# Conv attention on one core: q and k weights on the SP queue, idle products from a tile of ones, and a different split of the last group between ScalarE and VectorE

## The chip, the core and the metric

The kernel runs on one core of a Trainium2 chip. A core has five engines with instruction streams of their own: TensorE (PE, with PEld for its weight loads), VectorE (DVE), ScalarE (ACT), GpSimd (POOL) and SyncE (SP, which here only starts transfers). The metric is the device time of one execution in microseconds. The kernel before takes 2464.09 us (median of 5 runs, 2462.86 to 2464.92).

## The reference

For each of B = 4 images x of 64 x 64 positions and C = 256 channels, three linear maps are followed by an attention and a residual:

```python
q = jnp.einsum('bwhc,cd->bwhd', x, Wq) + bq      # 128 channels
k = jnp.einsum('bwhc,cd->bwhd', x, Wk) + bk      # 128 channels
v = jnp.einsum('bwhc,cd->bwhd', x, Wv) + bv      # 256 channels
pq = q.reshape(B, -1, N); pk = k.reshape(B, -1, N); pv = v.reshape(B, -1, N)   # N = 4096
energy = jnp.einsum('bcn,bcm->bnm', pq, pk)
attention = jax.nn.softmax(energy, axis=-1)
out = jnp.einsum('bcm,bnm->bcn', pv, attention)
return gamma * out.reshape(B, W, H, C) + x
```

The reshape is not a transpose: the rows of pq are made of 32 positions times 128 channels, so N = 4096 counts both.

## The kernel before, in words

**Setup (lines 85 to 102 and 187 to 199).** `ident`, the identity for transposes on PE, is built by POOL; `ones` is set by DVE. The weights of q and k share one tile, `wqk_sb`, which two transfers issued by ACT fill (lines 90 and 91). POOL issues the broadcasts of the two biases, the weights of v, the bias of v and gamma. Lines 196 to 199 let PE do 12 transposes of the identity into a PSUM tile `wp` that nobody reads.

**Order.** From line 201 on the order is written out by hand (`manual_schedule`): each engine carries out its instructions in the order of the program, and a semaphore holds an instruction until its data or its buffer is there. Generators (`finish`, `guard`) spread a piece of work over the loop: each `yield` gives way to the next step.

**Projection of an image (class Projection, lines 104 to 173).** x comes in 16 tiles of 256 KB, each 128 partitions by 2 by 256, loaded by SP into a pool of three buffers. `transposed(i)` first asks for tiles i and i + 1 (`load` starts a transfer only once per tile), then transposes tile i with four PE transposes (line 124), and ACT copies the result from PSUM (line 130). `qk(i)` multiplies it by `wqk_sb` (line 137), and DVE adds the biases (line 146). `v(i)` does the same for v. Of the first image, tiles 0 and 1 are transposed before the first `qk` (lines 483 to 485).

**Attention.** Each image has NG = 16 groups of 256 columns, and each group 8 steps. A step forms energies (line 324), their exponentials on ACT (line 328) in two factors that DVE multiplies (line 338), splits the product into parts `h`, `l` and `d`, and accumulates on PE (line 374): `h` and `l` into two accumulators `acc[0]` and `acc[1]`, 128 x 258 each, and `d` into the tile `bb`, whose two halves of 128 x 256 share one PSUM bank. Column C of an accumulator holds z, the sum by which the row is divided.

**End of a group.** `finish` writes z into `zall`, forms gamma * (1 + E) / z, adds `bb`, scales on ACT, transposes back on PE, and DVE adds the result to x before POOL stores it. The very last group goes through `finish_last` instead: DVE copies z of both accumulators, `factors` forms r = gamma / z, and `ra` = r (1 + E). For each half, ACT computes `bb` * r, DVE `acc` * ra + that (line 449), PE transposes it (line 454), and DVE adds it to x (line 459); SP stores (line 460). In between, `guard` looks at all z: two DVE operations test them against Z_LOW and Z_HIGH, a reduction and a product with `ones` on PE bring the partitions together, and DVE writes the flag `again`.

**After the last group.** Every engine loads `again` (line 547) and branches: if some z was out of range, a general kernel computes everything anew. With these inputs the branch is not taken. Then all engines meet at the closing barrier (line 672).

Of the kernel before, what the change touches and what calls it, by code (L numbers as in the profile page):

```python
# [9 lines left out]
F32 = mybir.dt.float32  # L10
F32R = mybir.dt.float32r
I32 = mybir.dt.int32
AF = mybir.ActivationFunctionType
ALU = mybir.AluOpType
# [6 lines left out]
def kernel(  # L21
# [36 lines left out]
    nc = tc.nc  # L58
    B, W, H, C = x.shape
    P = 128  # L60
    N = W * H
    C2 = C // 2
# [3 lines left out]
    Z_LOW, Z_HIGH = 2.0**-60, 2.0**80  # L66
# [20 lines left out]
    ones = const.tile([P, P], F32, name="ones")  # L87
    nc.vector.memset(ones, 1.0)
    wqk_sb = const.tile([P, KC, 2 * C2], F32, name="wqk_sb")
    nc.scalar.dma_start(wqk_sb[:, :, :C2], wq.rearrange("(k p) d -> p k d", p=P))  # L90
    nc.scalar.dma_start(wqk_sb[:, :, C2:], wk.rearrange("(k p) d -> p k d", p=P))
    bqk_sb = const.tile([P, 2 * C2], F32, name="bqk_sb")
    nc.gpsimd.dma_start(bqk_sb[:, :C2], bq.partition_broadcast(P))
    nc.gpsimd.dma_start(bqk_sb[:, C2:], bk.partition_broadcast(P))
# [100 lines left out]

    with tc.tile_pool(name="ps_w", bufs=1, space=PSUM) as ps_w:
        wp = ps_w.tile([P, P], F32, name="wp")
        for _ in range(12):
            nc.tensor.transpose(wp, ident, ident)

    with ExitStack() as fast:
        fast.enter_context(tc.manual_schedule())
# [181 lines left out]
                for j in range(NJ):  # L384
                    nc.scalar.activation(o[:, j, :], acc[j], AF.Identity, scale=1.0 + E)

        def factors(b, g, gamma):

            r = work.tile([P, 2, NJ], F32, tag="r", name=f"r_{b}_{g}")
            nc.vector.reciprocal(r[:, 0, :], zall[:, b * NG + g, :])  # L390
            nc.vector.tensor_tensor(r[:, 0, :], r[:, 0, :], gamma.to_broadcast([P, NJ]), ALU.mult)
            return r[:, 0, :], r[:, 1, :]

        def finish(b, g, o, bb, xr):
            yield
            yield

            nc.vector.tensor_copy(zall[:, b * NG + g, :], o[:, :, C])
            r, _ = factors(b, g, gam1)
            nc.vector.tensor_tensor(o[:, :, :C], o[:, :, :C], bb, ALU.add)  # L400
            yield
            for j in range(NJ):
                nc.scalar.activation(
                    o[:, j, :C], o[:, j, :C], AF.Identity, scale=r[:, j : j + 1]
                )
            yield
            yield
            tp = ps_t.tile([P, 2, NB], F32, tag="t", name=f"ot_{b}_{g}")
            for s in range(2):
                for j in range(NJ):  # L410
                    nc.tensor.transpose(
                        tp[:, s, j * P : (j + 1) * P], o[:, j, s * P : (s + 1) * P], ident
                    )
            yield
            nc.vector.tensor_tensor(xr, xr, tp, ALU.add)
            nc.gpsimd.dma_start(ov[b, g], xr)

        def guard():

            z = zall.rearrange("p n j -> p (n j)")  # L420
            ok = ppool.tile([P, 4, NB], F32, tag="y", name="ok")[:, 0, : B * NG * NJ]
            nc.vector.tensor_scalar(ok, z, Z_LOW, None, ALU.is_ge)
            nc.vector.scalar_tensor_tensor(ok, z, Z_HIGH, ok, ALU.is_le, ALU.mult)
            yield
            nc.vector.tensor_reduce(zs, ok, AX.X, ALU.min)
            nc.vector.tensor_scalar(zs, zs, 0.5, None, ALU.is_lt)
            zp = ps_s.tile([P, 1], F32, tag="b", name="zp")
            nc.tensor.matmul(zp, ones, zs, start=True, stop=True)
            yield
            nc.vector.tensor_copy(again, zp)  # L430
            yield
            yield

        def finish_last(b, g, xr):

            for j in range(NJ):
                a = now["acc"][j]
                nc.vector.tensor_copy(zall[:, b * NG + g, j : j + 1], a[:, C : C + 1])
            r, ra = factors(b, g, gam)
            check = guard()  # L440
            nc.vector.tensor_scalar(ra, r, 1.0 + E, None, ALU.mult)
            o = work.tile([P, NJ, C + 2], F32, tag="o", name=f"o_{b}_{g}")
            tps = []
            for j in range(NJ):
                next(check)
                nc.scalar.activation(
                    o[:, j, :C], now["bb"][:, j, :], AF.Identity, scale=r[:, j : j + 1]
                )
                nc.vector.scalar_tensor_tensor(
                    o[:, j, :C], now["acc"][j][:, :C], ra[:, j : j + 1], o[:, j, :C], ALU.mult, ALU.add  # L450
                )
                tp = (ps_t, ps_s)[j].tile([P, 2, P], F32, tag="ta"[j], name=f"ot_{b}_{g}_{j}")
                for s in range(2):
                    nc.tensor.transpose(tp[:, s, :], o[:, j, s * P : (s + 1) * P], ident)
                tps.append(tp)
            for j in range(NJ):
                next(check)
                n = slice(j * P, (j + 1) * P)
                nc.vector.tensor_tensor(xr[:, :, n], xr[:, :, n], tps[j], ALU.add)
            nc.sync.dma_start(ov[b, g], xr)  # L460

        def begin(b, i):
# [16 lines left out]
        for b in range(B):  # L479
            pr = images[b]  # L480
            if b == 0:
                now["banks"] = energies
                pr.transposed(0)
                pr.transposed(1)
                project_qk(b, 0)
            for i in range(1, NI):
# [189 lines left out]
```

## Time and profile before

| what | value |
|---|---|
| median of 5 runs | 2464.09 us (2462.86 to 2464.92) |
| the profiled execution's own time | 2463.21 us |
| its span, first to last instruction | 2461.3 us |
| start of the first product with `wqk_sb` (line 137) | 8.57 us |
| start of the last store (line 460) | 2453.69 us |
| moved by the DMA engines | 498.92 MB, mean 203 GB/s |

Times in the views are microseconds from the start of the span. A line of the timeline has the start, the length, the engine, the line of the kernel, the operation, output <- input, and how many instructions are merged; in brackets stands how long the engine was idle before it and what ended that. An engine name with a q at its end is the engine's own sequencer, which issues transfers and handles semaphores; that is not counted as busy. A busy PE means that matmuls follow each other; an fp32 product takes two passes, so it has two records. A view of one line lists its operations with the minimum, median and maximum duration in ns and the first and last start.

### The profile page before, as it was taken

The page shows a single profiled execution, that of the slowest core. Times are in us where ns is not written, and L with a number is a line of the kernel's source. Part 1 is how long each engine was busy: PE and PEld are TensorE (multiplying, and loading weights), DVE is VectorE, ACT ScalarE, POOL GpSimd, SP SyncE. Part 2 cuts the span into 40 slices and gives each one's busy share as a digit, 9 for nine tenths or more (in the row PEclk, how much of TensorE's full clock was granted, in tenths as well). Part 3 has the DMA queues.
Part 4 walks back from the last instruction along what each step waited for, and adds up shares of the span by engine and source line. Part 5 has one row for each costly group of instructions (what it writes and reads, how often), then busy time and mean ns, then how long its engine had stood idle before and what let it go on. Part 6 is the DMA issues. An engine that isn't in the chain of part 4 may idle for free.

```text
span 2461.3 us, 50024 instructions
## 1 busy us (share of the span) xinstructions
PE 2442.9 (99%) x19982; PEld 2408.9 (98%) x19982; DVE 2096.2 (85%) x2314; ACT 1804.2 (73%) x3201; POOL 425.7 (17%) x781
## 2 busy tenths in 40 slices
PE   9999999999999999999999999999999999999998
PEld 8999999999899999999989999999998999999998
DVE  5888888888698888888869888888876988888887
ACT  5777777776677777777667777777766777777775
POOL 4211111111411111111141111111114111111110
PEclk9999999999999999999999999999999999999999
DMA  7666666664766666666477666666647766666663
GB/s 231 217 205 209 206 204 203 203 215 152 228 221 197 209 206 204 211 196 213 140 239 220 203 200 211 203 209 200 208 141 239 222 209 197 209 203 210 204 201 112
DMA packets 137408, 498.92 MB, mean 203 GB/s; under 512 B 15536, under 2 KB 57264, under 8 KB 137168
## 3 DMA queue, kind: packets, MB, share of 16 engines
q0 software_dynamic: 92320, 453.17, 59.3%
q1 hardware_dynamic: 44304, 42.22, 5.6%
q8 instruction: 160, 2.62, 0.4%
q14 instruction: 80, 0.66, 0.1%
q10 hardware_dynamic: 544, 0.26, 0.0%
HBM read 445.25 MB, written 50.33 MB: 201 GB/s over the span
## 4 chain that ended last, share of the span: by engine, by line


## 5 line engine op out<-in xcount | busy, mean ns | idle before, releaser
L328 ACT ACTIVATE x<-sa 128x512 f32<-128x512 f32 x1024 | 612.7, 598 | 496.5 <-PE sa L324 493.3
L338 DVE TENSOR_TENSOR x<-x,y 128x1024 f32<-128x1024 f32 x512 | 626.2, 1223 | 187.9 <-ACT y L328 187.9
L324 PE MATMUL sa<-q,k 128*128 128x256 f32 x4096 | 736.6, 279 | 1.1 <-ACT x L328 1.0
L352 DVE SCALAR_TENSOR_TENSOR d<-h,x 128x1024 fp32r<-128x1024 f32 x512 | 624.0, 1219 | 0.0
L349 DVE TENSOR_TENSOR l<-x,h 128x1024 fp32r<-128x1024 f32 x512 | 624.0, 1219 | 0.0
L324 PEld LDWEIGHTS sa<-q,k 128*128 128x128 f32 x4096 | 619.5, 188 | 2.6 <-ACT x L328 2.0
L328 ACT ACTIVATE y<-sb 128x512 f32<-128x512 f32 x1024 | 614.3, 600 | 0.0
L374 PE MATMUL a<-vh,h 128*128 128x258 f32 x4096 | 574.4, 283 | 0.0
L374 PE MATMUL a<-vl,l 128*128 128x258 f32 x4096 | 572.8, 282 | 0.0
L324 PE MATMUL sb<-q,k 128*128 128x256 f32 x2048 | 567.5, 277 | 0.0
L343 ACT ACTIVATE h<-x 128x1024 fp32r<-128x1024 f32 x512 | 543.7, 1062 | 22.7 <-DVE x L338 19.2
L374 PE MATMUL bb<-vd,d 128*128 128x256 f32 x4096 | 558.6, 279 | 0.0
L308 POOL DMA_DIRECT2D k<-kf x512 | 280.0, 547 | 1575.5 <-PE sb L324 1550.6
L374 PEld LDWEIGHTS a<-vl,l 128*128 128x128 f32 x4096 | 525.3, 189 | 0.0
L374 PEld LDWEIGHTS a<-vh,h 128*128 128x128 f32 x4096 | 522.9, 189 | 0.0
L374 PEld LDWEIGHTS bb<-vd,d 128*128 128x128 f32 x4096 | 515.1, 188 | 0.0
L324 PEld LDWEIGHTS sb<-q,k 128*128 128x128 f32 x2048 | 384.5, 188 | 0.9 <-ACT y L328 0.8
L137 PE MATMUL qk<-wqk_sb,xts 128*128 128x256 f32 x512 | 121.0, 379 | 0.0
L158 PE MATMUL v<-xts,wv_sb 128*128 128x256 f32 x512 | 120.3, 379 | 0.0
L158 PEld LDWEIGHTS v<-xts,wv_sb 128*128 128x128 f32 x512 | 97.3, 190 | 13.2
L137 PEld LDWEIGHTS qk<-wqk_sb,xts 128*128 128x128 f32 x512 | 92.3, 190 | 10.0
L273 POOL DMA_DIRECT2D qd<-qks x128 | 69.1, 545 | 183.1 <-DVE qks L146 173.7
(56 smaller groups left out, 868.0 us busy)
## 6 DMA issues: line engine op xcount, KB each, us to landing
k<-kf POOLq DMA_DIRECT2D x512, 768.0 KB, 4.7
x<-in_x_dram SPq DMA_DIRECT2D x128, 256.0 KB, 3.5
kf<-f POOLq DMA_DIRECT2D x64, 384.0 KB, 3.7
out_dram<-x POOLq DMA_DIRECT2D x63, 256.0 KB, 2.6
qd<-qks POOLq DMA_DIRECT2D x128, 64.0 KB, 2.8
qr<-qd SPq DMA_DIRECT2D x64, 128.0 KB, 2.6
wv_sb<-in_L_conv_Wv_dram POOLq DMA_DIRECT2D x1, 256.0 KB, 7.3
out_dram<-x SPq DMA_DIRECT2D x1, 256.0 KB, 3.9
```

Source lines behind the costliest of these rows:

```text
L137: nc.tensor.matmul(qk[:, s, :], self.xt[i][:, k, s, :], wqk_sb[:, k, :], start=(k == 0), stop=(k == KC - 1),)
L158: nc.tensor.matmul(vp[:, eh, :], wv_sb[:, k, eh * P : (eh + 1) * P], self.xt[i][:, k].rearrange("p s a -> p (s a)"), start=(k == 0), stop= ...
L273: nc.gpsimd.dma_start(qd[b, i // 2 + NG // 2 * s][:, i % 2, :], x[:, s, :C2])
L308: nc.gpsimd.dma_start(t.rearrange("p (i s) f d -> p i s (f d)", s=2), kf[b, u % NU])
L324: nc.tensor.matmul(to[:, i], kt[:, 2 * k + i, f, :], q[:, f], start=first, stop=last)
L328: nc.scalar.activation(to[:, 2 * k : 2 * k + 2, :], sp.rearrange("p i j d -> p i (j d)"), AF.Exp, scale=scale,)
L338: nc.vector.tensor_tensor(x, x, y, ALU.mult)
L343: nc.scalar.activation(h, units[b, u], AF.Identity, scale=UPPER)
L349: nc.vector.tensor_tensor(l, x, h.bitcast(F32), ALU.subtract)
L352: nc.vector.scalar_tensor_tensor(d, h.bitcast(F32), 1.0 + E, x, ALU.mult, ALU.subtract)
L374: nc.tensor.matmul(out_, left[:, i, j * P : (j + 1) * P], right[:, m, : out_.shape[1]], start=(t == i == 0 and (left is h or left is d and ...
```

## The change

The two transfers of `wqk_sb` leave ACT's queue for SP's, behind the first tile of x, which is now asked for explicitly, and ahead of the second. The 12 transposes of the identity become 7 products of `ones` with itself, and two more such products follow the transposes of the first tile of x, in the bank that `ps_t` owns. `factors` goes, and `finish` has its two instructions in place.

In `finish_last` each accumulator gets its own reciprocal, `raj` = gamma (1 + E) / z and `rj` = gamma / z; ACT scales the accumulator by `raj`, and DVE afterwards adds `bb` * `rj`. The copies of z into `zall` come after that. `guard` is no generator any more: POOL clamps z between Z_LOW and Z_HIGH, DVE compares the clamped values with z, the reduction and the product follow, and `again` is written by one comparison, between the two final additions.

```diff
-    nc.scalar.dma_start(wqk_sb[:, :, :C2], wq.rearrange("(k p) d -> p k d", p=P))
-    nc.scalar.dma_start(wqk_sb[:, :, C2:], wk.rearrange("(k p) d -> p k d", p=P))
...
         wp = ps_w.tile([P, P], F32, name="wp")
-        for _ in range(12):
-            nc.tensor.transpose(wp, ident, ident)
+        for _ in range(7):
+            nc.tensor.matmul(wp, ones, ones, start=True, stop=True)
...
-        def factors(b, g, gamma):
-
-            r = work.tile([P, 2, NJ], F32, tag="r", name=f"r_{b}_{g}")
-            nc.vector.reciprocal(r[:, 0, :], zall[:, b * NG + g, :])
-            nc.vector.tensor_tensor(r[:, 0, :], r[:, 0, :], gamma.to_broadcast([P, NJ]), ALU.mult)
-            return r[:, 0, :], r[:, 1, :]
-
         def finish(b, g, o, bb, xr):
...
-            r, _ = factors(b, g, gam1)
+            r = work.tile([P, 2, NJ], F32, tag="r", name=f"r_{b}_{g}")[:, 0, :]
+            nc.vector.reciprocal(r, zall[:, b * NG + g, :])
+            nc.vector.tensor_tensor(r, r, gam1.to_broadcast([P, NJ]), ALU.mult)
...
             ok = ppool.tile([P, 4, NB], F32, tag="y", name="ok")[:, 0, : B * NG * NJ]
-            nc.vector.tensor_scalar(ok, z, Z_LOW, None, ALU.is_ge)
-            nc.vector.scalar_tensor_tensor(ok, z, Z_HIGH, ok, ALU.is_le, ALU.mult)
-            yield
+            nc.gpsimd.tensor_scalar(ok, z, Z_LOW, Z_HIGH, ALU.max, ALU.min)
+            nc.vector.tensor_tensor(ok, ok, z, ALU.is_equal)
             nc.vector.tensor_reduce(zs, ok, AX.X, ALU.min)
-            nc.vector.tensor_scalar(zs, zs, 0.5, None, ALU.is_lt)
             zp = ps_s.tile([P, 1], F32, tag="b", name="zp")
             nc.tensor.matmul(zp, ones, zs, start=True, stop=True)
-            yield
-            nc.vector.tensor_copy(again, zp)
-            yield
-            yield
+            return zp

         def finish_last(b, g, xr):

+            r = work.tile([P, 2, NJ], F32, tag="r", name=f"r_{b}_{g}")
+            o = work.tile([P, NJ, C + 2], F32, tag="o", name=f"o_{b}_{g}")
+            acc, bb = now["acc"], now["bb"]
             for j in range(NJ):
-                a = now["acc"][j]
-                nc.vector.tensor_copy(zall[:, b * NG + g, j : j + 1], a[:, C : C + 1])
-            r, ra = factors(b, g, gam)
-            check = guard()
-            nc.vector.tensor_scalar(ra, r, 1.0 + E, None, ALU.mult)
-            o = work.tile([P, NJ, C + 2], F32, tag="o", name=f"o_{b}_{g}")
+                rj, raj, z = r[:, 0, j : j + 1], r[:, 1, j : j + 1], acc[j][:, C : C + 1]
+                nc.vector.reciprocal(rj, z)
+                nc.vector.tensor_tensor(raj, rj, gam1, ALU.mult)
+                nc.scalar.activation(o[:, j, :C], acc[j][:, :C], AF.Identity, scale=raj)
+                nc.vector.tensor_tensor(rj, rj, gam, ALU.mult)
+            for j in range(NJ):
+                nc.vector.tensor_copy(zall[:, b * NG + g, j : j + 1], acc[j][:, C : C + 1])
             tps = []
             for j in range(NJ):
-                next(check)
-                nc.scalar.activation(
-                    o[:, j, :C], now["bb"][:, j, :], AF.Identity, scale=r[:, j : j + 1]
-                )
                 nc.vector.scalar_tensor_tensor(
-                    o[:, j, :C], now["acc"][j][:, :C], ra[:, j : j + 1], o[:, j, :C], ALU.mult, ALU.add
+                    o[:, j, :C], bb[:, j, :], r[:, 0, j : j + 1], o[:, j, :C], ALU.mult, ALU.add
                 )
...
+            zp = guard()
             for j in range(NJ):
-                next(check)
                 n = slice(j * P, (j + 1) * P)
                 nc.vector.tensor_tensor(xr[:, :, n], xr[:, :, n], tps[j], ALU.add)
+                if j == 0:
+                    nc.vector.tensor_scalar(again, zp, P - 0.5, None, ALU.is_lt)
             nc.sync.dma_start(ov[b, g], xr)
...
                 now["banks"] = energies
+                pr.load(0)
+                nc.sync.dma_start(wqk_sb[:, :, :C2], wq.rearrange("(k p) d -> p k d", p=P))
+                nc.sync.dma_start(wqk_sb[:, :, C2:], wk.rearrange("(k p) d -> p k d", p=P))
                 pr.transposed(0)
+
+                wp = ps_t.tile([P, P], F32, tag="t", name="wp1")
+                for _ in range(2):
+                    nc.tensor.matmul(wp, ones, ones, start=True, stop=True)
                 pr.transposed(1)
```

## The prediction, made before the result was known

> **What bounds the kernel now.** I read the page's busy times, then PE's waits, then the two ends in order of time, because the change touches only the first 10 us and the last 12.
>
> ```profile
> PE 2442.9 (99%) x19982; PEld 2408.9 (98%) x19982; DVE 2096.2 (85%) x2314; ACT 1804.2 (73%) x3201; POOL 425.7 (17%) x781
> ```
>
> PE works without a break; the waits of PE (total, times, longest) say where it does not:
>
> ```profile
> PE wp L199 <- POOL ident masks.py:199: 2.4, 1, 2.4
> PE xt L124 <- DMA x<-in_x_dram: 1.8, 1, 1.8
> PE ot L454 <- DVE o L449: 1.1, 1, 1.1
> ```
>
> So three pieces add up: the time until PE has the second tile of x, the matmuls from there to the last one of line 374, which the change leaves alone, and the tail. The start, in order of time (start, length, engine, line):
>
> ```profile
> 0.73 0.42 ACTq L90 DMA_DIRECT2D wqk_sb<-in_L_conv_Wq_dram  x1
> 1.19 0.49 ACTq L91 DMA_DIRECT2D wqk_sb<-in_L_conv_Wk_dram  x1
> 2.43 2.82 PE L199 MATMUL wp<-ident 128*128 128x128 f32 x12 [2.43 <-POOL ident masks.py:199]
> 5.31 0.94 PE L124 MATMUL xt<-ident,x 128*128 128x128 f32 x4
> 8.08 0.66 PE L124 MATMUL xt<-ident,x 128*128 128x128 f32 x4 [1.83 <-DMA x<-in_x_dram]
> 8.57 1.89 PE L137 MATMUL qk<-wqk_sb,xts 128*128 128x256 f32 x8
> ```
>
> PE idles from 6.25 to 8.07 and then never for long. What ends that wait is x1, the second tile, neither the weights nor the warm-up: SP issued the first three tiles at 0.73, 1.48 and 2.11, and they landed 3.9, 6.6 and 7.4 us later, at 4.6, 8.05 and 9.5. The DMA engines over that time (PE, PEld, DVE, ACT, POOL busy; PE clock; DMA share; GB/s):
>
> ```profile
> 2.37:3.50 1.13, 1.07 (x5) 1.07 (x6) 0.00 (x0) 1.01 (x3) 1.13 (x3) 1.00 0.88 274
> 3.50:4.00 0.50, 0.50 (x5) 0.50 (x4) 0.00 (x0) 0.00 (x0) 0.50 (x2) 1.00 0.65 189
> 4.00:8.05 4.05, 2.19 (x10) 1.55 (x8) 0.00 (x0) 0.59 (x1) 1.20 (x3) 1.00 0.90 202
> ```
>
> From 4.0 on they are 90% busy: x1 waits for bytes. The clock column reads 1.00 throughout, but the durations (minimum/median/maximum ns) show a slow clock at first:
>
> ```profile
> L199 PE MATMUL wp<-ident x12: 417/417/472, 2.4 to 4.8; 128*128 128x128 f32 x12
> ```
>
> ```profile
> L124 PE MATMUL xt<-ident,x x12: 272/273/474, 5.3 to 10.6; 128*128 128x128 f32 x12
> ```
>
> The same transpose takes 417 ns in the warm-up and 273 from the fourth one of x0 at 5.98 on. The tail:
>
> ```profile
> 2450.67 0.22 DVE L422 TENSOR_SCALAR ok<-zall 128x128 f32<-128x128 f32 x1
> 2450.93 0.84 ACT L446 ACTIVATE o<-bb,r 128x256 f32<-128x256 f32 x2 [6.76 <-PE bb L374]
> 2451.43 0.48 DVE L449 SCALAR_TENSOR_TENSOR o<-a,r,o 128x256 f32<-128x256 f32 x1 [0.21 <-ACT o L446]
> 2452.22 0.47 DVE L449 SCALAR_TENSOR_TENSOR o<-a,r,o 128x256 f32<-128x256 f32 x1
> 2452.83 0.16 DVE L430 CAST again<-zp 128x1 int32<-128x1 f32 x1
> 2452.91 0.75 DVE L459 TENSOR_TENSOR x<-x,ot 128x256 f32<-128x256 f32 x2
> 2453.69 0.60 SPq L460 DMA_DIRECT2D out_dram<-x  x1
> ```
>
> After the store comes what the busy times leave out, listed by line 672 (the end) and 547 (the load of the flag):
>
> ```profile
> L672 POOLq DRAIN  x3: 46/107/6683, 2453.8 to 2461.0; - x3
> L672 SPq DRAIN  x3: 7/7/13, 2459.3 to 2460.7; - x3
> ```
>
> ```profile
> L547 POOLq TENSOR_LOAD <-again x1: 486/486/486, 2453.0 to 2453.0; - x1
> ```
>
> POOL loads `again` at 2453.03, as soon as DVE has written it, branches, and sits from 2453.75 to 2460.44 in one drain; SP comes to its own drain at 2459.39. So POOL, not the store, arrives last at the closing barrier, 1.05 us after SP.
>
> **The change, start.** ACT loses two issues (0.42 + 0.49). Its table load moves from 1.71 to about 0.75, hidden: its next work that PE needs is the copy of x0's transposes at 6.29. SP gains both issues between x0 and x1, about 0.5 us each; behind them stand x1 and x2, so x1 is issued near 2.5 instead of 1.48. If x1 were bound by its issue, this costs 1.0 us. If it is bound by bytes, the same 768 KB (x0, both weights, x1) stand before its last byte as now. The packet records favour bytes: SP's queue had moved 258 KB by 4.0, x0 being 256, so x1, though issued at 1.48, did not start before about 4.0; an issue at 2.5 can still make that. From 4.0 to 5.0 some 38 KB of wk still compete with x1; at 202 GB/s that is 0.19 us, which now lies before 4.0. x1 lands 0.2 earlier. Ends: +1.0 (issue-bound) and -0.57, as x2 (9.5) then stops PE, which asks for it at 10.09. I take -0.2, nearest to the 90% row.
>
> The Trainium skill speaks against this edit: "DMA: Bandwidth & Descriptors", under "Issuing engines are not separate DMA queues", says that DMAs of all issuers interleave on the same engines and that several issuers save only issue time. The trace agrees that they interleave. By the rule alone the move gives up 1.0 us of SP's time for nothing, 2465.1; by the rows x1's issue has that much slack.
>
> **The idle products.** Seven products need the ones, ready at 1.00 (memset at 0.83, 0.17 long), where the transposes waited for the identity until 2.43. An fp32 product is two passes (line 137 has 512 records for 256 calls); at the warm-up's spacing of 0.213 us fourteen passes last from 1.03 to 4.2. x0, without wq beside it, is there by about then; its transposes run at 4.3 instead of 5.31 and the two further products (4 passes, 0.9) until 6.1, before x1. All of it lies in PE's idle time: cost 0, and if x1 came before 6.1 the difference would be paid. The slow clock is the risk: were it still slow at 8.07, work would take twice as long until it rises. The warm-up's 3.8 us (2.43 to 6.25) sufficed in the profiled execution; the new one is busy for nearly 5 (1.03 to 6.1), so I take 0, with +1.7 as the far end (the 3.5 us from 2.43 to 5.98 once more, half lost).
>
> The skill's "TensorE: Matmul & The Clock Gate", under "Part 4: PE-mode transpose", says that transposes do not count as busy for the gate. Here the trace disagrees: before 5.98 PE did nothing else, and the clock rose. By the rule the old warm-up was worthless and products would win time; by the row 8.08 is already at full speed and they win none.
>
> **The change, tail.** Sums and scales now come per accumulator, before bb is done. Accumulator 0 is ready for DVE at 2449.53, the other at 2450.01, bb for its reader at 2450.93 (starts of the first waiters). Dependent small DVE operations are 0.20 apart, independent ones 0.08. Reciprocal 2449.53, factor 2449.72 to 2449.88, ACT's scaling 2449.93 to 2450.40 (0.474); the second 2450.01, 2450.20, ACT 2450.40 to 2450.87. All lies under the matmuls of bb. The two copies into zall read banks that ACT reads; that they wait for ACT puts the second at 2450.91, that they do not at 2450.44; I take the wait, which costs 0.06. DVE's two combining operations then run at 2450.99 and 2451.39 (spacing 0.40) against 2451.43 and 2452.22: 0.44 and 0.83 earlier.
>
> The flag now comes behind them. POOL clamps 128x128 meanwhile from 2451.10; before has POOL's 128x2 scalar operation at 0.227 and a 128x128 select at 0.320; I take 0.35. DVE's comparison stands at 2451.79, so there is 0.66 of cover; beyond that each microsecond is paid, because the reduction, both adds and the store queue behind it. Bounds 0.23 and 1.0: 0 to +0.35. Comparison 0.29, reduction from 2452.12 to 2452.40, then 0.50 as now (2452.30 to 2452.83) through PE: `again` at about 2452.92. The first add fits in between (2452.32); the second now queues behind that wait and starts at 2453.00 instead of 2453.25. The store leaves 0.25 earlier, but POOL's load of `again` comes at 2453.08 instead of 2453.03. If the 6.68 us drain runs from there, the end moves by +0.05; if it follows the store, by -0.25. I take +0.05: POOL is the row that arrives last.
>
> **Sum.** The profiled execution took 2463.21 (span 2461.3 and 1.9 around it): -0.2 + 0 + 0.05 gives 2463.06. It lies 0.88 under the median of the five, 2464.09, which spread over 2.1 us. If that spread stays, the new median is 2463.94; if it came from late clocks that the longer warm-up mends, 2463.06. I take the middle, **2463.5**, 0.02% faster: no change by the 0.2% (4.9 us) that a measurement of this kernel can tell from none.
>
> **Rivals.** (a) Slower: x1 lands later. Place: SP's queue, where x1 now follows two transfers; it decides once x1 lands after 8.05, and costs up to 1.2 against my sum: with the spread of now, 2463.94 + 1.2 = 2465.1. For it: x1 is issued 1.0 later, and broadcasts of the biases hold engines at 4 to 7 us. Against it: x1's late first byte. (b) The clock is late: up to 1.7 more, 2463.94 + 1.7 = 2465.6. Against it: more PE work, earlier. (c) Both ends give what they can: x1 0.57 earlier and a drain that follows the store, -0.82: 2462.4, or 2462.0 beside the lowest run, 0.35 under the profiled one. (d) The loop does not stay: PE's stream grows by 12 instructions (24 become 36), so its instruction fetches (the page has 160 packets on q8) fall elsewhere; one matmul slot lost or won at each (eight matmuls of line 374 start within 0.95 us, 0.12 each) is 19 us, 2483 or 2444. Against it: no PE wait of this kind shows.
>
> **How the numbers follow.** Forecast 0.58, (a) 0.20, (b) 0.05, (c) 0.10, (d) 0.07 (0.04 slower, 0.03 faster). Only (d) passes 0.2%, so same is 0.93. The range runs from (c) beside the lowest run to (b), 2462.0 to 2465.6; (d) is left out.
>
> **What would show it.** Right: line 137's first matmul at about 8.4, x0's transposes near 4.3, transposes of x1 at 273 ns; DVE's last add near 2453.0 counted from the same last matmul; POOL's drain again near 6.7 us and last. Wrong: SP's x1 landing after 8.1, x1's transposes at 417 ns, the comparison waiting for POOL, or a drain that ends with the store.

## The result, and the profile after

The changed kernel takes 2466.84 us (median of 24 runs, 2465.86 to 2468.34), the kernel before beside it 2464.50 (44 runs, 2462.03 to 2466.31). The ratio is 1.0012, with a 95% interval of 1.0006 to 1.0017: 2.3 us slower, which is less than the 0.2% that counted as a difference here, and still outside the predicted range of 2462.0 to 2465.6.

The profiled execution took 2466.19 us with a span of 2464.1, against 2463.21 and 2461.3 before. Its pieces, measured at the same events in both traces:

| piece | before | after | difference |
|---|---|---|---|
| start of the span to the transposes of x1 | 8.08 | 9.40 | +1.32 |
| from there to the transposes of the third tile, x2 | 2.22 | 3.67 | +1.45 |
| from there to the start of the last `bb` matmul | 2440.31 | 2440.13 | -0.18 |
| from there to the end of the span | 10.68 | 10.91 | +0.22 |

The four differences add up to the 2.8 us of the spans (the times of the two executions differ by 2.98; 0.2 of that lies outside the spans, where no view looks). So the start holds the loss, the loop lost nothing, and the tail a little.

PE's waits after (total, times, longest). The wait for x1, 1.8 us before, is now 3.3; the warm-up's wait, 2.4 before, is 1.1, as the change lets it start from the ones:

```profile
PE xt L122 <- DMA x<-in_x_dram: 3.3, 1, 3.3
PE wp L197 <- DVE ones L88: 1.1, 1, 1.1
```

The start in order of time (start, length, engine, line), first SP's queue, then PE:

```profile
0.74 0.68 SPq L82 DMA_DIRECT2D x<-in_x_dram  x1
1.48 0.58 SPq L474 DMA_DIRECT2D wqk_sb<-in_L_conv_Wq_dram  x1
2.10 0.47 SPq L475 DMA_DIRECT2D wqk_sb<-in_L_conv_Wk_dram  x1
2.62 11.62 SPq L82 DMA_DIRECT2D x<-in_x_dram  x5
```

```profile
4.51 1.09 PE L122 MATMUL xt<-ident,x 128*128 128x128 f32 x4
5.39 0.69 PE L480 MATMUL wp<-ones 128*128 128x128 f32 x4
9.40 1.11 PE L122 MATMUL xt<-ident,x 128*128 128x128 f32 x4 [3.32 <-DMA x<-in_x_dram]
10.31 2.92 PE L135 MATMUL qk<-wqk_sb,xts 128*128 128x256 f32 x8
13.07 0.60 PE L122 MATMUL xt<-ident,x 128*128 128x128 f32 x4
```

x1 is issued at 2.62 and lands at 9.36. PE has nothing from 6.08 to 9.40. Then the four transposes take 1.11 us where the third tile's, at 13.07, take 0.60, and the first eight matmuls of line 135 take 2.92 us where they took 1.89 before. That is a slow clock, and here the clock column (the seventh value) shows it:

```profile
5.60:8.90 3.30, 0.48 (x4) 0.29 (x3) 0.00 (x0) 0.59 (x1) 0.00 (x0) 1.00 0.90 255
9.00:12.30 3.30, 2.90 (x9) 2.52 (x10) 0.00 (x0) 0.59 (x1) 0.46 (x2) 0.50 0.37 108
12.50:15.50 3.00, 3.00 (x18) 2.64 (x17) 1.52 (x4) 0.89 (x2) 1.15 (x2) 1.00 0.24 73
```

After a stretch of 3.3 us in which PE was busy for only 0.48, it is granted half its clock from 8.97 to 12.39. Before, its clock rose at 5.94 and stayed: its gap was 1.83 us.

The DMA engines over the same three stretches as in the prediction (engines' busy time, clock, DMA share, GB/s; a packet's whole time is counted where it starts, so that a share can pass 1):

```profile
2.37:3.50 1.13, 1.13 (x7) 1.13 (x7) 0.00 (x0) 0.05 (x1) 1.13 (x3) 1.00 1.14 255
3.50:4.00 0.50, 0.50 (x5) 0.50 (x3) 0.00 (x0) 0.00 (x0) 0.50 (x2) 1.00 1.57 153
4.00:8.05 4.05, 1.98 (x10) 1.52 (x9) 0.00 (x0) 0.59 (x1) 1.27 (x3) 1.00 0.84 180
```

From 3.5 to 4.0 the packets that start take more engine time than the stretch has, and move fewer bytes than before (153 GB/s, then 189). So a busy engine is not a measure of bytes moved. Whose packets these are, the records of POOL's queue tell: those of 4096 bytes that start between 3 and 7 us, 34 of them, last 1.00 us on average and up to 1.95, 34.1 us of engine time in sum (before: 39, mean 0.56, up to 1.71, sum 21.9). The two broadcasts make 32 packets of that size (2 x 64 KB); the first 32 of the queue last 1.06 us on average after the change and 0.64 before it, and those behind them, of `wv_sb`, mostly 0.16. The queue's part of the first 12 us in the table of queues (packets, MB, share of 16 engines), after:

```profile
q0 software_dynamic: 240, 0.40, 23.7%
```

Before, the same 240 packets and 0.40 MB had 17.4%. POOL's queue carries the two broadcasts of the biases, `wv_sb`, and two small loads. The same broadcasts thus hold the engines for longer once the weights stand behind x0, and over the three stretches together all queues move 1.09 MB where they moved 1.22 before.

The tail, in order of time (in brackets: how long the engine was idle and what ended that):

```profile
2453.08 0.16 DVE L434 COPY zall<-a 128x1 f32<-128x1 f32 x1
2453.56 0.16 DVE L434 COPY zall<-a 128x1 f32<-128x1 f32 x1 [0.32 <-ACT o L431]
2453.63 0.87 DVE L437 SCALAR_TENSOR_TENSOR o<-bb,r,o 128x256 f32<-128x256 f32 x2
2453.81 0.65 POOL L415 TENSOR_SCALAR ok<-zall 128x128 f32<-128x128 f32 x1 [19.73 <-DVE zall L434]
2454.49 0.29 DVE L416 TENSOR_TENSOR ok<-ok,zall 128x128 f32<-128x128 f32 x1
2455.64 0.16 DVE L449 TENSOR_SCALAR again<-zp 128x1 int32<-128x1 f32 x1 [0.21 <-PE zp L419]
2456.16 0.60 SPq L450 DMA_DIRECT2D out_dram<-x  x1
```

```profile
L669 POOLq DRAIN  x3: 46/107/6683, 2456.6 to 2463.8; - x3
L669 SPq DRAIN  x3: 7/7/13, 2461.9 to 2463.5; - x3
```

Counted from the last `bb` matmul's start (2450.61 before, 2453.20 after), the store is issued at +2.96 instead of +3.08, and `again` is written at +2.44 instead of +2.22. POOL's drain of 6683 ns starts later by the same 0.2, and the end with it, +0.22, although the store was earlier; SP comes to its drain at 2461.9, before POOL's is over (2463.3, where POOL's next entry at this line starts).

### The profile page after: what moved, and what is told of

Same layout as the page of the kernel before. It is cut to its first block, busy times and chain, and to the rows that moved or that the text cites. A ratio compares the mean times of both kernels' runs of the same rounds, so it can differ in the third digit from the quotient of the medians.

```text
span 2464.1 us, 50040 instructions
## 1 busy us (share of the span) xinstructions
PE 2445.4 (99%) x19988; PEld 2411.5 (98%) x19988; DVE 2096.1 (85%) x2315; ACT 1803.9 (73%) x3201; POOL 426.5 (17%) x782
## 3 DMA queue, kind: packets, MB, share of 16 engines
q8 instruction: 160, 2.62, 0.4%
## 4 chain that ended last, share of the span: by engine, by line
PE 96%; ACT 2%; DVE 1%; issue 0%; DMA 0%; SPq 0%; ACTq 0%; DVEq 0%
PE a L372 39%; PE bb L372 19%; PE sa L322 18%; PE sb L322 9%; PE qk L135 5%; PE v L156 4%; PE ot L404 1%; PE xt L122 1%; ACT h L341 1%; DVE x L336 1%; ACT x L326 0%; ACT y L326 0%; DMA x<-in_x_dram 0%; DVE vd L289 0%; ACT vh L286 0%
```

## The experiments

All of them compute the full result. "Lands" is the end of the transfer of x1 in the profile. Ratios are to the kernel before, run beside them.

My theory was the **place in the queue**: x1 lands late because it stands behind the weights in SP's queue, and the longer gap lets the clock fall. The rivals: the **clock** alone, which the changed warm-up fails to hold whatever the queue does, and the **tail**. The first four runs separate them.

**Weights back on ACT**, the rest of the change kept:

```diff
     wqk_sb = const.tile([P, KC, 2 * C2], F32, name="wqk_sb")
+    nc.scalar.dma_start(wqk_sb[:, :, :C2], wq.rearrange("(k p) d -> p k d", p=P))
+    nc.scalar.dma_start(wqk_sb[:, :, C2:], wk.rearrange("(k p) d -> p k d", p=P))
...
-                pr.load(0)
-                nc.sync.dma_start(wqk_sb[:, :, :C2], wq.rearrange("(k p) d -> p k d", p=P))
-                nc.sync.dma_start(wqk_sb[:, :, C2:], wk.rearrange("(k p) d -> p k d", p=P))
                 pr.transposed(0)
```

> The changed kernel with the two loads of the q and k weights back on ACT's queue; idle products and tail as changed. Queue theory (x1 stands behind the weights on SP's queue and lands 1.3 us late, and the longer gap on PE then lets the clock fall, another 1.45 us): x1 lands near 8.05, x1's transposes take 273 ns, time 2464.0 to 2464.8, the tail's +0.2 included. Warm-up theory (the idle products, starting 1.4 us earlier, end too early, so the clock falls whatever the queue): x1 near 8.05, but its transposes at 417 ns, about 2466. Tail theory (the cost sits after the last matmul): unchanged, 2466.8.

Measured: 2464.74 (2462.26 to 2466.42), ratio 1.0002 (0.9993 to 1.0011). x1 lands at 7.57. PE in the profiled execution, one of the low ones (2462.41):

```profile
7.62 0.66 PE L124 MATMUL xt<-ident,x 128*128 128x128 f32 x4 [1.17 <-DMA x<-in_x_dram]
8.11 1.89 PE L137 MATMUL qk<-wqk_sb,xts 128*128 128x256 f32 x8
```

Its times lie in two groups, five between 2462.3 and 2463.1, six between 2464.7 and 2466.4. With the weights on ACT the loss is gone as far as the interval can tell (0.66 above the kernel before beside it), and the tail of the change is still in: the tail falls as the main cause.

**Only the weights moved**, in the kernel before:

```diff
     wqk_sb = const.tile([P, KC, 2 * C2], F32, name="wqk_sb")
-    nc.scalar.dma_start(wqk_sb[:, :, :C2], wq.rearrange("(k p) d -> p k d", p=P))
-    nc.scalar.dma_start(wqk_sb[:, :, C2:], wk.rearrange("(k p) d -> p k d", p=P))
...
                 now["banks"] = energies
+                pr.load(0)
+                nc.sync.dma_start(wqk_sb[:, :, :C2], wq.rearrange("(k p) d -> p k d", p=P))
+                nc.sync.dma_start(wqk_sb[:, :, C2:], wk.rearrange("(k p) d -> p k d", p=P))
                 pr.transposed(0)
```

> The kernel before with only the two loads of the q and k weights moved to SP behind the first x. Queue theory: x1 lands near 9.4 and the time is 2465.8 (x1 alone) to 2467.2 (x1 and a clock that falls in the gap). Warm-up theory: x1 late but no fall of the clock, 2465.8. Tail theory: 2464.5.

Measured: 2466.16 (2465.11 to 2467.06), ratio 1.0008 (0.9999 to 1.0017). PE:

```profile
8.61 1.11 PE L122 MATMUL xt<-ident,x 128*128 128x128 f32 x4 [2.18 <-DMA x<-in_x_dram]
9.51 3.62 PE L135 MATMUL qk<-wqk_sb,xts 128*128 128x256 f32 x8
```

Moving the weights alone brings 2.1 of the 2.3 us, with the old warm-up and the old tail. The interval still touches 1; what carries the reading is that all eleven times lie above 2465.1, as only 6 of the 33 of the kernel before do. In this execution the clock was not up until 14.45.

**Fifteen products instead of two** after the transposes of x0, which leaves the queue as changed and fills PE's gap:

```diff
-                for _ in range(2):
+                for _ in range(15):
                     nc.tensor.matmul(wp, ones, ones, start=True, stop=True)
```

> The changed kernel with 15 idle products in place of 2 between the transposes of x0 and x1, so that PE is busy until about 9. Queue theory: x1 still lands near 9.4, but its transposes take 273 ns and the first product with the q and k weights starts at about 9.8; 1.45 us less than the changed kernel, 2465.4. If the clock were not the second half of the cost: 2466.8, or more by what the products overrun.

Measured: 2464.86 (2464.28 to 2465.38), ratio 1.0003 (0.9994 to 1.0012). PE:

```profile
5.39 3.67 PE L480 MATMUL wp<-ones 128*128 128x128 f32 x30
9.11 0.66 PE L122 MATMUL xt<-ident,x 128*128 128x128 f32 x4
9.61 1.89 PE L135 MATMUL qk<-wqk_sb,xts 128*128 128x256 f32 x8
```

x1 still lands late, at 9.07, but the clock stays up, and the median is 2.0 below the changed kernel's. Taken against the kernel before beside each, the gain is 1.6 (0.8 above it instead of 2.3). So a large part of the loss is the clock; x1's delay stays, and the clock falls as the only cause.

**x1 ahead of the weights** in SP's queue:

```diff
                 pr.load(0)
+                pr.load(1)
                 nc.sync.dma_start(wqk_sb[:, :, :C2], wq.rearrange("(k p) d -> p k d", p=P))
```

> The changed kernel with SP issuing x0, x1, then the q and k weights. If the place in the queue is what delays x1: x1 lands at 6 to 7, and the weights, now last, land at 7 to 8.5, so the first product starts at 8 to 8.5 and the time is 2464 to 2465. If the bytes or the broadcasts of the biases set the pace whatever the order: whichever comes last of x1 and the weights still lands near 9.4 and the time stays within 0.7 of 2466.8.

Measured: 2465.73 (2463.68 to 2467.07), ratio 1.0008 (0.9999 to 1.0017), above what the place in the queue let expect. PE, and then the clock as above:

```profile
8.28 0.86 PE L122 MATMUL xt<-ident,x 128*128 128x128 f32 x4 [2.38 <-DMA x<-in_x_dram]
9.30 3.30 PE L135 MATMUL qk<-wqk_sb,xts 128*128 128x256 f32 x8 [0.15 <-DMA wqk_sb<-in_L_conv_Wk_dram]
```

```profile
5.20:8.50 3.30, 0.92 (x8) 0.73 (x7) 0.00 (x0) 0.59 (x1) 0.07 (x1) 1.00 0.87 243
8.70:11.90 3.20, 3.05 (x9) 2.23 (x8) 0.00 (x0) 0.59 (x1) 0.46 (x2) 0.50 0.48 151
```

x1 lands at 8.23, 1.13 earlier, but the weights now land last, at 8.62 and 9.16, and the gap of 2.38 is still long enough for the clock to fall. Something other than the order keeps this queue slow up to 8 us. The last of the four transfers lands at 9.16, near the 9.4 that the rival (bytes or broadcasts set the pace) expected, and the time lies between the two. A miss of the theory in its simple form, and the reason for the run with the biases below.

**Weights on ACT and nine products**, the two cures together:

```diff
+    nc.scalar.dma_start(wqk_sb[:, :, :C2], wq.rearrange("(k p) d -> p k d", p=P))
+    nc.scalar.dma_start(wqk_sb[:, :, C2:], wk.rearrange("(k p) d -> p k d", p=P))
...
-                pr.load(0)
-                nc.sync.dma_start(wqk_sb[:, :, :C2], wq.rearrange("(k p) d -> p k d", p=P))
-                nc.sync.dma_start(wqk_sb[:, :, C2:], wk.rearrange("(k p) d -> p k d", p=P))
...
-                for _ in range(2):
+                for _ in range(9):
```

> The changed kernel with the weights' loads back on ACT and 9 idle products in place of 2 behind the transposes of x0, so PE is busy from 1.05 until about 7.6, when x1 lands. Clock theory (the two groups of times that the kernel before and the run with the weights on ACT show, near 2462.7 and near 2465, are executions whose clock was up or down when x1 came): one group only, 2462.3 to 2463.3, with the changed tail's +0.2 included. If the two groups come from the landing of x1: both stay, median 2464 to 2465.

Measured: 2462.88 (2462.28 to 2463.73), ratio 0.9995 (0.9986 to 1.0004), one group. With the changed kernel this gives a table of medians:

| | PE's gap filled | PE's gap left |
|---|---|---|
| weights on ACT | 2462.88 | 2464.74 |
| weights on SP | 2464.86 | 2466.84 |

By these medians the queue costs 2.0 or 2.1, the gap 1.9 or 2.0. The four come from three sets of runs, whose kernel before read 2464.34, 2464.08 and 2464.50; taken against these, the queue costs 2.2 or 1.7 and the gap 2.1 or 1.6. So the two prices add up to within half a microsecond, but they are no independent mechanisms: with the weights on ACT five of the eleven times lie in the lower group although the gap is left, and by means instead of medians the gap costs 1.4 there. Nor do the profiles show all of the queue's price: with the gap filled x1's transposes start at 7.75 and 9.11, 1.36 apart.

**Does a filled gap mend the kernel before too?** Sixteen more transposes of the identity there, after the first tile's, of the kind that the old warm-up has:

```diff
                 pr.transposed(0)
+                wp = ps_t.tile([P, P], F32, tag="t", name="wp1")
+                for _ in range(16):
+                    nc.tensor.transpose(wp, ident, ident)
                 pr.transposed(1)
```

> The kernel before with 16 more transposes of the identity between the transposes of x0 and of x1, nothing else changed. If transposes count as activity for the clock: x1's transposes take 273 ns and the upper group of times goes, median near 2463, or up to 1.5 more where the transposes still run slowly and overrun x1. If they do not count: the two groups stay or the time grows, 2464.5 to 2466.

Measured: 2463.45 (2462.91 to 2463.92), ratio 0.9998 (0.9989 to 1.0007). PE:

```profile
6.21 2.14 PE L486 MATMUL wp<-ident 128*128 128x128 f32 x16
8.19 0.60 PE L124 MATMUL xt<-ident,x 128*128 128x128 f32 x4
```

The kernel before has 19 runs from 2462.0 to 2463.5 and 25 from 2464.1 to 2466.3; with the gap filled the upper group is empty, in this run as in the one with nine products (none of either's 11 lies above 2464.0, where 19 of the 33 of the kernel before beside them do). In the sets of the experiments the two groups are less clearly parted: 10 of the 93 times of the kernel before lie between 2463.5 and 2464.1. The groups are thus the clock, up or down when x1 comes, as far as this can be read without a profile of an execution in before's upper group, which there is not. It also shows that transposes hold the clock: in this profile it rises at 6.67 after nothing but transposes and stays up. They run until 8.19, 0.67 past the landing of x1 at 7.52, so x1 waits for them.

**The biases last**: the order of SP's queue as changed, but POOL issues the two broadcasts after its other loads:

```diff
     bqk_sb = const.tile([P, 2 * C2], F32, name="bqk_sb")
-    nc.gpsimd.dma_start(bqk_sb[:, :C2], bq.partition_broadcast(P))
-    nc.gpsimd.dma_start(bqk_sb[:, C2:], bk.partition_broadcast(P))
...
     nc.gpsimd.dma_start(gam, gamma.partition_broadcast(P))
+    nc.gpsimd.dma_start(bqk_sb[:, :C2], bq.partition_broadcast(P))
+    nc.gpsimd.dma_start(bqk_sb[:, C2:], bk.partition_broadcast(P))
```

> The changed kernel with the two broadcasts of the biases issued by POOL behind the weights of v, its bias and gamma, not ahead of them. Broadcast theory (x1 is late because the broadcasts' packets, up to 2 us each, hold the DMA engines at 3.5 to 7 us, and behind the weights on SP's queue x1 meets all of them): x1 lands at 6 to 7.5, time 2464 to 2465.5. Queue-only theory (x1 is late because its issue and the bytes ahead of it are late): x1 still lands near 9, 2466.8.

Measured: 2462.46 (2461.93 to 2464.44), ratio 0.9996 (0.9987 to 1.0005), better than expected, and with an interval wholly below that of the changed kernel. Seven times lie at 2462.57 or below and four from 2463.5 to 2464.4, so some executions may still lose the clock in the gap of 1.46. The engines from 3.5 to 4.0, and PE:

```profile
3.50:4.00 0.50, 0.50 (x5) 0.50 (x3) 0.00 (x0) 0.00 (x0) 0.50 (x2) 1.00 1.17 437
```

```profile
6.90 0.65 PE L122 MATMUL xt<-ident,x 128*128 128x128 f32 x4 [1.46 <-DMA x<-in_x_dram]
7.39 1.89 PE L135 MATMUL qk<-wqk_sb,xts 128*128 128x256 f32 x8
```

Where the changed kernel moves 153 GB/s this one moves 437, at a smaller share. The packets of POOL's queue that start between 3 and 7 us, mostly those of `wv_sb` now, take 0.18 us on average instead of 1.00. x1, still behind the weights, lands at 6.86 instead of 9.36. How much of x had landed, or was under way, by the packet records (KB; x0 is the first 256):

| by | before | after | biases last |
|---|---|---|---|
| 4 us | 258 | 256 | 297 |
| 5 us | 385 | 256 | 551 |
| 6 us | 454 | 256 | 760 |
| 7 us | 605 | 392 | 768 |

So the changed kernel's x1 gets no byte before 6 us, and what holds it back are the packets of the broadcasts, with the weights first in line for what is left.

**The same in the kernel before**, nothing else changed there:

```diff
-    nc.gpsimd.dma_start(bqk_sb[:, :C2], bq.partition_broadcast(P))
-    nc.gpsimd.dma_start(bqk_sb[:, C2:], bk.partition_broadcast(P))
...
     nc.gpsimd.dma_start(gam, gamma.partition_broadcast(P))
+    nc.gpsimd.dma_start(bqk_sb[:, :C2], bq.partition_broadcast(P))
+    nc.gpsimd.dma_start(bqk_sb[:, C2:], bk.partition_broadcast(P))
```

> The kernel before with only the two bias broadcasts moved behind the weights of v, its bias and gamma. Broadcast theory: x1 lands at 6 to 7.2 instead of 8.05, so PE's gap behind the transposes of x0 shrinks to about 1 us and the clock stays up more often: median 2462 to 2463. If the broadcasts matter only behind the weights: 2464.3.

Measured: 2461.81 (2461.43 to 2463.73), ratio 0.9990 (0.9981 to 0.9999). x1 lands at 7.02, a microsecond before its time in the kernel before. The profiled execution is the slowest of the eleven, 2463.73, and shows a late clock once more:

```profile
7.06 1.11 PE L124 MATMUL xt<-ident,x 128*128 128x128 f32 x4 [0.44 <-DMA x<-in_x_dram]
7.97 3.47 PE L137 MATMUL qk<-wqk_sb,xts 128*128 128x256 f32 x8
```

Nine of the eleven lie at 2462.07 or below, two at 2463.62 and 2463.73: here a profile has caught an execution of the upper group, and its clock is late.

**The tail: an early flag.** The drain theory: the end follows from when POOL has loaded `again`, because its last drain takes a fixed time. The store theory: it follows the store. The kernel with nine products, with the z of all older groups tested on DVE before the last matmuls, and only the two newest after their reciprocals:

```diff
+            nc.vector.tensor_scalar(ok[:, :n0], z[:, :n0], Z_LOW, Z_HIGH, ALU.max, ALU.min)
+            nc.vector.tensor_tensor(ok[:, :n0], ok[:, :n0], z[:, :n0], ALU.is_equal)
+            nc.vector.tensor_reduce(ok[:, n0 + 2 :], ok[:, :n0], AX.X, ALU.min)
...
+            nc.vector.tensor_scalar(ok[:, n0 : n0 + 2], z[:, n0:], Z_LOW, Z_HIGH, ALU.max, ALU.min)
+            nc.vector.tensor_tensor(ok[:, n0 : n0 + 2], ok[:, n0 : n0 + 2], z[:, n0:], ALU.is_equal)
+            nc.vector.tensor_reduce(zs, ok[:, n0:], AX.X, ALU.min)
+            zp = ps_s.tile([P, 1], F32, tag="b", name="zp")
+            nc.tensor.matmul(zp, ones, zs, start=True, stop=True)
...
-            zp = guard()
             for j in range(NJ):
                 n = slice(j * P, (j + 1) * P)
-                nc.vector.tensor_tensor(xr[:, :, n], xr[:, :, n], tps[j], ALU.add)
                 if j == 0:
                     nc.vector.tensor_scalar(again, zp, P - 0.5, None, ALU.is_lt)
+                nc.vector.tensor_tensor(xr[:, :, n], xr[:, :, n], tps[j], ALU.add)
```

> The run with the weights on ACT and 9 products, and with the check of z moved forward: VectorE tests the 126 older values before the last matmuls end, the last two as soon as they are known, and the flag is written ahead of the two final additions; POOL does none of it. Drain theory (the end follows POOL's load of the flag by a fixed time, 6.68 us of drain among it): the flag is written 1.1 after the last matmul starts instead of 2.4, the end comes at +9.6 to +9.8 instead of +10.9, time 2461.2 to 2462.2. Store theory (the end follows the store): the store leaves at about +2.2 instead of +2.96 and the end moves by that, +10.1.

Measured: 2461.80 (2461.18 to 2462.50), ratio 0.9990 (0.9981 to 0.9999). DVE's last operations, and the drain:

```profile
2451.55 0.15 DVE L448 TENSOR_SCALAR again<-zp 128x1 int32<-128x1 f32 x1
2451.77 0.81 DVE L449 TENSOR_TENSOR x<-x,ot 128x256 f32<-128x256 f32 x2
```

```profile
L666 POOLq DRAIN  x3: 46/107/6683, 2452.5 to 2459.7; - x3
```

From the last `bb` matmul, `again` is at +1.19 instead of +2.44, and the end at +9.65 instead of +10.91: 1.25 and 1.26. The drain is 6683 ns again, though it starts before the store now. The drain theory holds.

**All of it together**, once with the weights on ACT, once on SP: the biases last, six products, the early flag. Against the kernel with the early flag:

```diff
     bqk_sb = const.tile([P, 2 * C2], F32, name="bqk_sb")
-    nc.gpsimd.dma_start(bqk_sb[:, :C2], bq.partition_broadcast(P))
-    nc.gpsimd.dma_start(bqk_sb[:, C2:], bk.partition_broadcast(P))
...
     nc.gpsimd.dma_start(gam, gamma.partition_broadcast(P))
+    nc.gpsimd.dma_start(bqk_sb[:, :C2], bq.partition_broadcast(P))
+    nc.gpsimd.dma_start(bqk_sb[:, C2:], bk.partition_broadcast(P))
...
-                for _ in range(9):
+                for _ in range(6):
```

> Weights on ACT, biases behind the weights of v on POOL, 6 idle products behind the transposes of x0, and the early flag. Broadcast theory: with the broadcasts gone from 3.5 to 7 us x1 lands at 6 to 7, one group of times, 2460.0 to 2461.5. If the broadcasts only matter to an x1 that stands behind the weights: x1 near 7.5 to 8 as with the weights on ACT before, 2461.8.

Measured: 2461.15 (2459.92 to 2462.07), ratio 0.9988 (0.9979 to 0.9997), the lowest median of all, 2.9 below the kernel before and 5.7 below the changed one. PE:

```profile
5.20 1.50 PE L477 MATMUL wp<-ones 128*128 128x128 f32 x12
6.54 0.60 PE L124 MATMUL xt<-ident,x 128*128 128x128 f32 x4
6.98 1.89 PE L137 MATMUL qk<-wqk_sb,xts 128*128 128x256 f32 x8
```

The other has the weights where the change puts them:

```diff
-    nc.scalar.dma_start(wqk_sb[:, :, :C2], wq.rearrange("(k p) d -> p k d", p=P))
-    nc.scalar.dma_start(wqk_sb[:, :, C2:], wk.rearrange("(k p) d -> p k d", p=P))
...
+                pr.load(0)
+                nc.sync.dma_start(wqk_sb[:, :, :C2], wq.rearrange("(k p) d -> p k d", p=P))
+                nc.sync.dma_start(wqk_sb[:, :, C2:], wk.rearrange("(k p) d -> p k d", p=P))
```

> The same with the q and k weights on SP behind x0, as in the changed kernel. Broadcast theory: with the broadcasts out of the way the queue of the weights matters little, x1 near 6.9, within 0.5 us of the run with the weights on ACT. Queue-only theory: x1 later by the 1.1 us by which SP issues it later, 1 us slower than the run with the weights on ACT.

Measured: 2461.88 (2461.02 to 2462.12), ratio 0.9990 (0.9981 to 0.9999). x1 lands at 7.23 instead of 6.24, and the median is 0.73 higher, between the two expectations (0.5 and 1 us). The intervals overlap, but five of the eleven times with the weights on ACT lie below the lowest with the weights on SP, and the spans of the profiles differ by 0.66. In both, the products end a little after x1 has landed, so its transposes start at 6.54 and 7.43.

A landing is that of one execution, and it scatters. x1's in all thirteen profiles, save the one with x1 ahead of the weights:

| | weights on ACT | weights on SP |
|---|---|---|
| biases first | 7.52, 7.52, 7.57, 8.03, 8.16 | 8.56, 9.07, 9.36 |
| biases last | 6.24, 7.02 | 6.86, 7.23 |

With the biases first the two orders are apart, by 1.2 us on average; with the biases last they overlap, and 0.4 is left. The place in the queue thus delays x1 where the broadcasts hold the engines. What it costs by itself the landings cannot tell from their scatter; the 0.73 between the medians is the better figure.

## Why the prediction was wrong, point by point

**"From 4.0 on they are 90% busy: x1 waits for bytes."** The failing step. The share was read as bytes: the sum took the engines to be moving x1 and its forerunners at the speed of the stretch, so that the order would not matter. Neither held. The engines were in good part taken by the packets of the broadcasts, which last about 1 us and carry 4 KB. With those moved away, x1 lands 2.5 us earlier at the same order of queue. That the same 768 KB stand before x1's last byte in either order was right, but not all of them were ahead of x1 before: the weights came over another queue and x moved beside them, 385 KB of x by 5 us against 256 now. Why the broadcasts' packets themselves take longer with the weights on SP (1.06, 1.07 and 1.10 us on average in three profiles, 0.64 to 0.79 in five with the weights on ACT) stays open.

**x1 lands 0.2 earlier, at most 1.0 later.** It landed 1.3 later in the profile, at 9.36, past the 8.1 that the prediction named as a sign of being wrong. The upper end was the time that SP spends on two more issues; x1's issue did move by 1.14 (from 1.48 to 2.62). That the issue alone decides is excluded by the run with the biases last, where x1, behind the same two weights, lands 2.5 earlier than in the changed kernel. The prediction had the right mechanism in rival (a), with its two ingredients, the place in the queue and the broadcasts at 4 to 7 us, and gave it 0.20. "x1's late first byte", its argument against it, told only that x0's bytes stood ahead of x1's in the same queue; with both weights ahead as well, the first byte of x1 moved from 3.98 to 6.22.

**The Trainium skill, "DMA: Bandwidth & Descriptors", under "Issuing engines are not separate DMA queues".** By that rule alone the move was a loss of 1.0, 2465.1, and the text preferred the row. The sign and roughly the size of x1's delay are on the rule's side (1.32 in the profile). It doesn't tell the rest: that one and the same move delays x1 by 1.2 us on average with the broadcasts in front, and by 0.4, within the scatter, without them.

**The idle products: cost 0, clock risk 0.** The products were where they were said to be, from 1.05, and x0's transposes at 4.51 (4.3 predicted). The clock step failed: the text asked whether the clock would rise in time, not whether it could fall again before x1. It had risen at 5.56 and fell at 8.97, after a window in which PE was busy for 15% of the time, and cost 1.45. The far end, +1.7, covered the size. But rivals (a) and (b) were given chances as if independent and the range took only the dearer of them, while here one cause brings both: x1 late makes the gap longer, and the gap costs the clock. The two profile terms together are 2.77, and the range had room for 1.7.

**Transposes and the clock gate** (the Trainium skill, "TensorE: Matmul & The Clock Gate", under "Part 4: PE-mode transpose"). The prediction went by the row, that the clock rises after nothing but transposes, against the rule that they don't count. The run with sixteen more transposes bears the row out for these fp32 transposes: its times lose their upper group as those with products do.

**The middle of 2463.06 and 2463.94, as the longer warm-up might mend late clocks.** It did not: with weights on ACT and two products, the same longer warm-up, the times still have both groups, with nine products only the lower. What mends them is work in the gap before x1, not work before x0.

**The tail: `again` at +0.05, the drain follows POOL.** The mechanism was right, and the sign against the store's gain too: the store left 0.12 earlier and the end came 0.22 later. The sizes: the clamp on POOL took 0.65, not 0.35. The cover of 0.66 was just used up: the comparison starts 0.03 after the clamp ends (2454.46 and 2454.49). The second copy into `zall` did wait for ACT, as taken, but ACT was done 0.07 later than worked out. Counted from the last `bb` matmul, the comparison was expected at +1.18 and came at +1.29, and `again` was expected at +2.31 and came at +2.44: 0.13 of small terms that the sum had too short.

**The loop does not stay (rival d).** It stayed: -0.18 over 2440 us.

**No measurable difference by 0.2%, chance 0.93.** That held; the number inside it did not.

## What to carry to other kernels

A high busy share of the DMA engines is not a transfer rate: put the bytes beside it and look for the queue whose packets are slow, because a broadcast of 64 KB can stand before the tile that the first matmul needs, and a load moved behind others in its queue pays more for it (here 1.2 us with the broadcasts in front, 0.4 to 0.7 without). At the start of a kernel, count what a late tile does to PE's clock as well as to its wait, in one rival, and fill the gap with idle matmuls. At the end, find the engine whose last fixed piece starts latest, here POOL's drain behind the branch on a flag, and bring forward what releases it rather than the last store.

## What the runs showed of the hardware

- **The clock moves in windows of 3.41 us** (half clock from 8.97 to 12.39 in the changed kernel, full from 5.56 to 8.97), whose position differs from run to run: the rise to full speed came at 3.98 to 6.86 us in eleven of the profiles here, at 11.16 and 14.45 in two. It rose after a window with PE busy 86% of the time (biases last, 0.57 to 3.98), and did not after one with 85% (the kernel before with biases last, 4.33 to 7.75). It fell after 15% (changed kernel) and 30% (x1 ahead of the weights), and stayed after 46% (kernel before). The ends of matmuls are modelled, so 85 and 86% are too close to tell a threshold between them. The clock fell with PE idle for no more than 2.38 us at a stretch (x1 ahead of the weights). A clock that is not up when x1 comes costs 1.4 to 2.1 us here (transposes of x1 to those of x2: 3.67 in the changed kernel, 4.32 with only the weights moved, 2.22 before).
- **Broadcasts to 128 partitions are slow per packet**: 0.64 us on average before and 1.06 after, up to 1.95, for 4096 bytes, where most of those of `wv_sb` of the same size take 0.16. Moved last, they are still slow, 0.88 to 1.18 in four profiles, with nothing urgent behind them. Why they are slow stays open.
- **POOL's last drain took 6683 ns in every profile**, wherever the store stood.
- **A clamp of 128x128 fp32 took 0.65 us on POOL**; the same clamp of 128x126 took 0.22 on DVE (early flag).

Open as well: how often the changed kernel loses its clock, as it has one profile; that its 24 times form one group, 2.5 us wide, suggests nearly always. And as x1's landing scatters by up to 0.8 between profiles with the same order, the split of 1.32 and 1.45 is that of one execution; that the loss comes from the queue and the clock together rests on the groups of times. Of the 2 us between the medians with the gap filled, the profiles place 1.4 before x1's transposes; the rest has no place in any of them.
